# Scan block of a state-space layer: input products of two chunks interleaved, and 13 instead of 9 of 32 output products on GpSimd

## The chip, the core and the metric

The kernel runs on one core of a Trainium2 chip, in fp32 throughout. A core has five engines that run their own instruction queues beside each other: TensorE (PE in the profile) for matrix products into PSUM, VectorE (DVE), ScalarE (ACT), GpSimd (POOL), and SyncE (SP), which here only issues DMA transfers. GpSimd reads and writes SBUF alone; VectorE and ScalarE reach PSUM too in this kernel. The metric is the time of one execution on the device in microseconds (us), the median of three runs.

## The reference

The input is x of 4 batches x 512 tokens x 256 features and a context of 4 x 64 x 192. Four layers follow each other: two blocks with cross attention (the second with self attention too), a selective state-space stack (four "mamba" blocks after 64 tokens made of the context), and a last attention block. The change lies in the third. With 512 inner channels e and 16 states s, each of its blocks computes, after an input projection, a short convolution and a silu that give xi:

```python
dt, Bm, Cm = jnp.split(xdbl, [DR_, DR_ + DS_], axis=-1)
dt = jax.nn.softplus(jnp.einsum('bsr,er->bse', dt, dtp_w) + dtp_b)
A = -jnp.exp(A_log)
dA = jnp.exp(dt[..., None] * A)
dBu = dt[..., None] * Bm[:, :, None, :] * xi[..., None]

def step(h, t):
    da, dbu, c = t
    h = da * h + dbu
    return (h, jnp.einsum('bes,bs->be', h, c))
```

so for every channel and state there is a first-order recurrence over 512 tokens, and the output sums h times C over the states.

## The kernel before, in words

The state-space stack is `layer2` (from L1364). Its work is cut in 16 units (4 blocks x 4 batches). A unit has four chunks of 128 channels, taken as two pairs of chunks; the channels lie on the 128 partitions and the tokens along the row. A pair is done in 16 steps: a step i handles one chunk k of the pair and two states, and `where(i)` gives unit, pair, pair of states s2 and chunk k. Steps with the same s2 follow each other, so that two neighbouring steps (i even, i odd) share the maps of two states. In all there are 512 steps.

Parts of one step, with the engine that runs each:

- `maps` (L1674) has SP load B (tile bB) and C (tile bC) of two states, spread to all partitions, 512 KB each, once per two steps. bB has three buffers, bC four; bB is asked for five steps ahead, bC four.
- `product` (L1681) on GpSimd multiplies dtx (dt times xi, one chunk) by bB into dBu, 2 x 511 elements a row (L1685): dtx is read twice, once per state, and every row of bB once. dBu has four buffers.
- `decay` (L1689) on ScalarE writes exp(dt A) to PSUM (ps_dA, two buffers), one instruction per state (L1697).
- `begin` (L1699) on ScalarE copies the state at token 0 into column 0 of dBu (L1702), for each step.
- `states` (L1704) on VectorE scans 1024 elements (L1712), from ps_dA and dBu.
- The output product h times bC is done either by VectorE in the same step (`outputs_here`, L1719, tile hC) or by GpSimd one step later (`outputs`, L1723, tile hP). `on_gpsimd` (L119) says which: of 32 steps, 9 go to GpSimd.
- `add_up` on PE adds the products into ps_y by transposing matmuls (L1745), two steps behind or, for GpSimd's, three. After 16 steps `close_pair` (L1755) on VectorE multiplies the sum by the gate.

The rest of a unit (projections, convolution, gate, output projection) is written as generators (`front`, `step`, `gate`, `gated`) that are advanced twice a step. `step` (L1538) prepares a pair: dt for two chunks, then for each chunk dtx (L1564) and a small chain h0, i0 for token 0 (L1566 to L1575). The order on every engine is the order in which the loop at the end of `layer2` issues the instructions; nothing is moved afterwards. A buffer of a tile is written again only when its last reader is done, and an engine whose next instruction waits for that stands still with all that is behind it in its queue.

The context, ctxT, is loaded once at the start (L135) by ScalarE's queue into a tile that stays for the whole program; the first two layers, the state-space prefix and the last layer read it.

Of the kernel before, what the change touches and what calls it, by code (L numbers as in the profile page):

```python
# [8 lines left out]
F32 = mybir.dt.float32  # L9
# [6 lines left out]
P = 128  # L16
# [101 lines left out]

def on_gpsimd(i):  # L119

    return i % 4 == 0 or i % 32 == 26


@with_exitstack
def kernel(ctx: ExitStack, tc: tile.TileContext, t: dict, out: bass.AP):
# [5 lines left out]
    cols = keep.tile([P, NCOL], F32, name="cols")  # L131
    nc.scalar.dma_start(out=cols, in_=t["cols"])

    ctxT = keep.tile([CP, 2, B, 2, S], F32, name="ctxT")
    nc.scalar.dma_start(out=ctxT, in_=t["ctxT"].rearrange("(c p) b r s -> p c b r s", p=CP))  # L135
    const = keep.tile([P, 1 + TPB], F32, name="const")
    mean_w, mhalf = const[:, 0:1], const[:, 1:]
    nc.gpsimd.memset(mean_w, 1.0 / D)
# [1225 lines left out]
    def layer2(hT, A, far, h63, tail, X, fw, wl, late):  # L1364
# [5 lines left out]
        with ExitStack() as st:  # L1370
# [167 lines left out]
            def step(n, pair):  # L1538


                l, b = divmod(n, B)
                q = units[n]
                while "fronted" not in q:
                    yield
                w, xd, xi, b0 = q["w"], q["xd"], q["xi"], q["b0"]
                ms = (2 * pair, 2 * pair + 1)
                dt2 = pool.tile([P, 2, T], F32, name="dt", tag="dt", bufs=2)
                for i, m in enumerate(ms):
                    yield from need(1, 0)
# [10 lines left out]
                q["got", pair] = got = []  # L1560
                for i, m in enumerate(ms):
                    dt = dt2[:, i, :]
                    dtx = pool.tile([P, T], F32, name="dtx", tag="dtx", bufs=4)
                    nc.gpsimd.tensor_mul(dtx, dt, xi[:, m, :])  # L1564
                    h0 = pool.tile([P, NS], F32, name="h0", tag="h0", bufs=4)
                    nc.scalar.activation(h0, A[:, l, m, :], AF.Exp, scale=dt[:, 0:1])  # L1566
                    yield
                    yield
                    i0 = pool.tile([P, NS], F32, name="i0", tag="i0", bufs=2)
                    nc.gpsimd.tensor_mul(i0, b0, dtx[:, 0:1].broadcast_to([P, NS]))  # L1570
                    nc.gpsimd.tensor_mul(h0, h0, h63[:, l, b, m, :])
                    nc.gpsimd.tensor_add(h0, h0, i0)
                    yield
                    yield
                    nc.scalar.copy(dt[:, 0:1], far)  # L1575
                    q["used0"] = q.get("used0", 0) + 1
                    got.append((dt, dtx, h0))
                    yield

            def gate(n):  # L1580

# [92 lines left out]
            def maps(i, k):  # L1674

                n, pair, s2, _ = where(i)
                tl = pool.tile([P, 2, T], F32, name=("bB", "bC")[k], tag=("bB", "bC")[k], bufs=3 + k)
                nc.sync.dma_start(out=tl, in_=units[n]["scr"][k, 2 * s2 : 2 * s2 + 2].partition_broadcast(P))
                bmap[i // 2, k] = tl

            def product(i):  # L1681
                n, pair, s2, k = where(i)
                dtx = units[n]["got", pair][k][1]
                dBus[i] = dBu = pool.tile([P, 2, T], F32, name="dBu", tag="dBu", bufs=4)
                nc.gpsimd.tensor_mul(  # L1685
                    dBu[:, :, 1:], dtx[:, 1:].unsqueeze(1).broadcast_to([P, 2, T - 1]), bmap[i // 2, 0][:, :, 1:]
                )

            def decay(i, j):  # L1689
                n, pair, s2, k = where(i)  # L1690
                l, b = divmod(n, B)
                m, s = 2 * pair + k, 2 * s2 + j
                if j == 0:
                    dAs[i] = psum.tile([P, 2, T], F32, name="ps_dA", tag="dA", bufs=2)
                dA = dAs[i][:, j, :]
                dt = units[n]["got", pair][k][0]
                nc.scalar.activation(dA, dt, AF.Exp, scale=A[:, l, m, s : s + 1])  # L1697

            def begin(i):  # L1699
                n, pair, s2, k = where(i)  # L1700
                h0 = units[n]["got", pair][k][2]
                nc.scalar.copy(dBus[i][:, :, 0], h0[:, 2 * s2 : 2 * s2 + 2])  # L1702

            def states(i):  # L1704
                if on_gpsimd(i):
                    hC = pool.tile([P, 2, T], F32, name="hP", tag="hP", bufs=2)
                else:
                    hC = pool.tile([P, 2, T], F32, name="hC", tag="hC", bufs=4)
                hCs[i] = hC
                dA = dAs[i].rearrange("p s t -> p (s t)")  # L1710
                to = hC.rearrange("p s t -> p (s t)") if on_gpsimd(i) else dA
                nc.vector.tensor_tensor_scan(  # L1712
                    to, dA, dBus.pop(i).rearrange("p s t -> p (s t)"), 0.0, ALU.mult, ALU.add
                )

            def outputs_here(i):
                dA = dAs.pop(i)
# [64 lines left out]
            with tc.manual_schedule():  # L1782
                for i in range(first, last):
# [18 lines left out]
                    if main and r in (10, 14):  # L1802
                        flush_silu()

                    for k, ahead in ((0, 5), (1, 4)):
                        j = i + ahead
                        if 0 <= j < NU * US and j % 2 == 1:
                            maps(j - 1, k)
# [6 lines left out]
                    if i == -1:  # L1815
                        product(0)
                        product(1)
                        begin(0)
                    if main and i + 2 < NU * US:
                        product(i + 2)  # L1820
                    if 0 <= i - 1 < NU * US:
                        outputs(i - 1)

# [16 lines left out]
                        advance()  # L1840
                    if main:
                        outputs_here(i)
                    if 1 <= i + 2 < NU * US:
                        begin(i + 2)
                    if not closing:
                        advance()
# [126 lines left out]

    with ExitStack() as st:
        predram = st.enter_context(tc.tile_pool(name="prescr", bufs=2, space=DRAM))
        wp = st.enter_context(tc.tile_pool(name="w8", bufs=4))
        xp = st.enter_context(tc.tile_pool(name="X1", bufs=1))
        X = xp.tile([P, NT, D], F32, name="X")
        side = Beside(st.enter_context(ExitStack()))
        layer0(X, wp, side)  # L1980
        w = {n: load_l1(wp, n) for n in ("Wq1", "Wk1", "Wv1", "Wo1")}
        layer1(X, wp, w, st, side, hT)
    with ExitStack() as st:
# [15 lines left out]
        layer2(hT, A, far[:, 0:1], h63, tail, X, fw, wl, late)  # L1999
        layer3(X, wa, wl)  # L2000


# [68 lines left out]
```

## Time and profile before

| | before |
|---|---|
| median of 3 runs | 4056.72 us (4055.46 to 4058.05) |
| profiled execution, first to last instruction | 4054.1 us |
| scans of the main loop, first to last start | 1593.2 to 3337.8 us |
| busy in the span: PE, DVE, ACT, POOL | 3472.6, 3010.6, 2183.2, 2430.7 us |
| input products on GpSimd, L1685 | 512 of 2364 ns |
| output products on GpSimd, L1723 | 144 of 2360 ns |
| scans on VectorE, L1712 | 512 of 2.28 us |
| output products on VectorE, L1719 | 368 of 1223 ns |
| loads bB and bC | 256 each, 512 KB, 3.7 and 4.4 us to landing |

The profiled execution's own total time is not recorded beside its span; the span is 2.6 us below the median of the runs. A row of a group reads: line, engine, operation, output<-inputs with partitions x elements, number of instructions, then busy time and mean duration, then the time that the engine sat idle before them and who ended that. Durations of neighbouring instructions of one engine overlap by some hundredths of a microsecond.

### The profile page before, as it was taken

How to read it: one execution, taken by the hardware profiler on the slowest of the kernel's cores; microseconds unless marked ns; L12 is line 12 of the kernel's file. 1: busy time of each engine (PE TensorE's matmuls, PEld its weight loads, DVE VectorE, ACT ScalarE, POOL GpSimd, SP SyncE). 2: the span in 40 equal slices, each digit the busy share in tenths (PEclk: the TensorE clock that was granted, in tenths of full speed). 3: DMA queues.
4: the chain of work that ended last, by engine and by line, in shares of the span. 5: the costliest groups of instructions: out<-in, count | busy, mean ns of one | idle time of the engine just before them, and what ended most of it. 6: DMA issues, size and time to landing. Idle time of an engine off the chain costs nothing. (4 is left out here: it accounts for less than half of the span.)

```text
span 4054.1 us, 48619 instructions
## 1 busy us (share of the span) xinstructions
PE 3472.6 (86%) x17616; PEld 2197.1 (54%) x17616; DVE 3010.6 (74%) x2885; ACT 2183.2 (54%) x4394; POOL 2430.7 (60%) x1649
## 2 busy tenths in 40 slices
PE   7989998998888897887888798888887668999889
PEld 4654554554565554555555565555555444555446
DVE  5547567566565642899999999999999996666653
ACT  2345455454322433676777767776776644556422
POOL 3349259077100424899999999999999971001121
PEclk9999999999998998888888888888888779999989
DMA  2023023023100112444454445444444431000000
GB/s 77 12 91 101 26 79 99 18 89 105 45 1 0 56 28 85 151 152 160 155 175 159 163 155 169 164 167 148 161 171 147 168 109 37 1 1 1 1 6 16
DMA packets 140287, 369.93 MB, mean 91 GB/s; under 512 B 20624, under 2 KB 38224, under 8 KB 140048
## 3 DMA queue, kind: packets, MB, share of 16 engines
q1 hardware_dynamic: 136688, 363.58, 27.1%
q10 hardware_dynamic: 3360, 3.25, 0.3%
q8 instruction: 139, 2.28, 0.2%
q14 instruction: 100, 0.82, 0.1%
HBM read 363.50 MB, written 3.28 MB: 90 GB/s over the span
## 5 line engine op out<-in xcount | busy, mean ns | idle before, releaser
L1685 POOL TENSOR_TENSOR dBu<-dtx,bB 128x1022 f32<-128x1022 f32 x512 | 1200.7, 2364 | 14.7 <-DVE ps_dA L1712 12.4
L1697 ACT ACTIVATE ps_dA<-dt,A 128x512 f32<-128x512 f32 x1024 | 708.0, 691 | 390.6 <-DVE hC L1719 336.1
L1712 DVE TENSOR_TENSOR_SCAN ps_dA<-ps_dA,dBu 128x1024 f32<-128x1024 f32 x368 | 840.4, 2284 | 26.4 <-ACT ps_dA L1697 20.5
L1019 ACT ACTIVATE pr<-ps_s,nm 128x512 f32<-128x512 f32 x512 | 345.2, 686 | 259.2 <-DVE nm L1015 259.2
L1745 PE MATMUL ps_y<-ident,hC 128*128 128x128 f32 x2944 | 420.3, 294 | 56.7 <-DVE hC L1719 56.3
L1719 DVE TENSOR_TENSOR hC<-ps_dA,bC 128x1024 f32<-128x1024 f32 x368 | 450.2, 1223 | 21.7 <-DVE ps_dA L1712 0.5
L1745 PEld LDWEIGHTS ps_y<-ident,hC 128*128 128x128 f32 x2944 | 372.0, 153 | 119.6 <-DVE hC L1719 81.0
L1015 DVE TENSOR_REDUCE nm<-ps_s 128x2 f32<-128x1024 f32 x256 | 301.3, 1218 | 159.0 <-PE ps_s L1004 144.7
L1712 DVE TENSOR_TENSOR_SCAN hP<-ps_dA,dBu 128x1024 f32<-128x1024 f32 x144 | 328.4, 2280 | 52.7 <-POOL dBu L1685 48.1
L1723 POOL TENSOR_TENSOR hP<-hP,bC 128x1024 f32<-128x1024 f32 x144 | 339.9, 2360 | 26.5 <-PE ps_y L1745 9.8
L1033 PE MATMUL ps_pt<-ident,pr 128*128 128x128 f32 x2048 | 285.2, 279 | 66.6 <-DVE pT L1038 34.7
L1033 PEld LDWEIGHTS ps_pt<-ident,pr 128*128 128x128 f32 x2048 | 233.1, 142 | 164.9 <-issue 61.4
L663 POOL TENSOR_TENSOR ln_rstd<-ln_rstd,const 128x4 f32<-128x4 f32 x24 | 24.4, 1019 | 445.3 <-DVE ln_rstd L662 443.7
L582 DVE TENSOR_TENSOR_SCAN phb<-pdA,phb 128x512 f32<-128x512 f32 x128 | 224.5, 1768 | 62.3 <-POOL phb L572 45.8
L178 PE MATMUL ps_cv<-xp,w_dg 128*128 128x512 f32 x512 | 240.9, 607 | 28.9 <-ACT dBu L1702 21.6
L1745 PE MATMUL ps_y<-ident,hP 128*128 128x128 f32 x1152 | 188.6, 318 | 86.8 <-POOL hP L1723 86.8
L1745 PEld LDWEIGHTS ps_y<-ident,hP 128*128 128x128 f32 x1152 | 164.7, 167 | 144.1 <-POOL hP L1723 95.3
L1036 ACT COPY pT<-ps_pt 128x512 f32<-128x512 f32 x256 | 140.7, 592 | 171.6 <-PE ps_pt L1033 171.0
L1052 PE MATMUL ps_o<-pT,V 128*64 128x256 f32 (+1 forms) x2048 | 220.5, 392 | 1.8 <-ACT AT L1070 1.8
L1004 PE MATMUL ps_s<-kT,qT 64*128 64x512 f32 (+1 forms) x1024 | 207.5, 643 | 2.2 <-DVE kT L1225 1.4
L572 POOL TENSOR_TENSOR phb<-hT_res,pm 128x512 f32<-128x512 f32 x128 | 188.2, 1475 | 32.8 <-DMA pm<-scrp 18.1
L835 POOL TENSOR_TENSOR pr<-pr,rs 128x512 f32<-128x512 f32 x64 | 65.4, 1043 | 219.2 <-DVE rs L833 201.0
(275 smaller groups left out, 6408.6 us busy)
## 6 DMA issues: line engine op xcount, KB each, us to landing
bB<-scr SPq DMA_DIRECT2D x256, 512.0 KB, 3.7
bC<-scr SPq DMA_DIRECT2D x256, 512.0 KB, 4.4
pm<-scrp SPq DMA_DIRECT2D x224, 256.0 KB, 3.1
w_pw_in<-in_L_in SPq DMA_DIRECT2D x7, 512.0 KB, 4.5
X<-in_x SPq DMA_DIRECT2D x4, 512.0 KB, 7.2
w_L_W<-in_L_W SPq DMA_DIRECT2D x2, 1024.0 KB, 10.1
w_L_Wq<-in_L_Wq SPq DMA_DIRECT2D x2, 1024.0 KB, 6.5
w_L_Wo<-in_L_Wo SPq DMA_DIRECT2D x2, 1024.0 KB, 8.9
```

The costliest lines, as they stand in the source:

```text
L178: nc.tensor.matmul(dst, l, r, start=(i == 0), stop=(i == len(pairs) - 1))
L582: nc.vector.tensor_tensor_scan(hb, dA, hb, 0.0, ALU.mult, ALU.add)
L1015: nc.vector.tensor_reduce(nm, ps, AX.X, ALU.max, negate=True)
L1019: nc.scalar.activation(pr, ps[:, x, :], AF.Exp, bias=nm[:, x : x + 1], accum_out=rs[:, y : y + 1])
L1033: nc.tensor.transpose(pp[:, t4, :], pr[:, t4 * P : (t4 + 1) * P], ident)
L1052: nc.tensor.matmul(ps_o[0][j * stride : (j + 1) * stride, half * W2 : (half + 1) * W2], Vs[n][0][:, t4, h * stride : (h + 1) * stride], pT ...
L1685: nc.gpsimd.tensor_mul(dBu[:, :, 1:], dtx[:, 1:].unsqueeze(1).broadcast_to([P, 2, T - 1]), bmap[i // 2, 0][:, :, 1:])
L1697: nc.scalar.activation(dA, dt, AF.Exp, scale=A[:, l, m, s : s + 1])
L1712: nc.vector.tensor_tensor_scan(to, dA, dBus.pop(i).rearrange("p s t -> p (s t)"), 0.0, ALU.mult, ALU.add)
L1719: nc.vector.tensor_mul(hCs[i], dA, bmap[i // 2, 1])
L1723: nc.gpsimd.tensor_mul(hCs[i], hCs[i], bmap[i // 2, 1])
L1745: nc.tensor.matmul(y[:, j, k * P : (k + 1) * P], hC[:, s, j * P : (j + 1) * P], ident, is_transpose=True, start=False, stop=(2 * s2 + s == ...
```

## The change

`product` writes the two chunks of a pair into one tile dBu[state, token, chunk], the chunk innermost: one GpSimd instruction still covers 1022 elements, now both chunks of one state instead of both states of one chunk. dtx holds both chunks side by side for each token, and bB is read with each of its elements twice. `step` makes dtx, h0 and i0 for both chunks in single instructions (h0's two exponentials stay two). The scan reads its half of dBu with a step of two elements. `begin` copies once per two steps. Products are issued three steps ahead instead of two, dBu has three buffers of a pair (formerly four of a step), bB two buffers and is asked for six steps ahead. GpSimd takes the output products of all even steps but 10, 20 and 30 of 32: 13 instead of 9. hP and hC share six buffers (formerly two and four). ctxT no longer stays for the whole program: it is loaded at the start for the first layers, and again for the last one, first on SP's queue there.

```diff
 def on_gpsimd(i):
-    return i % 4 == 0 or i % 32 == 26
+    return i % 2 == 0 and i % 32 not in (10, 20, 30)
...
-    ctxT = keep.tile([CP, 2, B, 2, S], F32, name="ctxT")
-    nc.scalar.dma_start(out=ctxT, in_=t["ctxT"].rearrange("(c p) b r s -> p c b r s", p=CP))
+    def load_contexts(pool, queue):
+        nonlocal ctxT
+        ctxT = pool.tile([CP, 2, B, 2, S], F32, name="ctxT")
+        queue.dma_start(out=ctxT, in_=t["ctxT"].rearrange("(c p) b r s -> p c b r s", p=CP))
...
+                dtx = pool.tile([P, T, 2], F32, name="dtx", tag="dtx", bufs=2)
+                nc.gpsimd.tensor_mul(dtx.rearrange("p t k -> p k t"), dt2, xi[:, ms[0] : ms[1] + 1, :])
+                h0 = pool.tile([P, 2, NS], F32, name="h0", tag="h0", bufs=2)
                 for i, m in enumerate(ms):
-                    dt = dt2[:, i, :]
-                    dtx = pool.tile([P, T], F32, name="dtx", tag="dtx", bufs=4)
-                    nc.gpsimd.tensor_mul(dtx, dt, xi[:, m, :])
-                    h0 = pool.tile([P, NS], F32, name="h0", tag="h0", bufs=4)
-                    nc.scalar.activation(h0, A[:, l, m, :], AF.Exp, scale=dt[:, 0:1])
...
+                    nc.scalar.activation(h0[:, i, :], A[:, l, m, :], AF.Exp, scale=dt2[:, i, 0:1])
...
+                i0 = pool.tile([P, 2, NS], F32, name="i0", tag="i0")
+                nc.gpsimd.tensor_mul(
+                    i0, b0.unsqueeze(1).broadcast_to([P, 2, NS]), dtx[:, 0, :].unsqueeze(2).broadcast_to([P, 2, NS])
+                )
+                nc.gpsimd.tensor_mul(h0, h0, h63[:, l, b, ms[0] : ms[1] + 1, :])
+                nc.gpsimd.tensor_add(h0, h0, i0)
...
             def maps(i, k):
...
-                tl = pool.tile([P, 2, T], F32, name=("bB", "bC")[k], tag=("bB", "bC")[k], bufs=3 + k)
+                tl = pool.tile([P, 2, T], F32, name=("bB", "bC")[k], tag=("bB", "bC")[k], bufs=2 + 2 * k)
...
             def product(i):
-                n, pair, s2, k = where(i)
-                dtx = units[n]["got", pair][k][1]
-                dBus[i] = dBu = pool.tile([P, 2, T], F32, name="dBu", tag="dBu", bufs=4)
+                n, pair, s2, j = where(i)
+                dtx = units[n]["got", pair][1]
+                if j == 0:
+                    dBus[i // 2] = pool.tile([P, 2, T, 2], F32, name="dBu", tag="dBu", bufs=3)
                 nc.gpsimd.tensor_mul(
-                    dBu[:, :, 1:], dtx[:, 1:].unsqueeze(1).broadcast_to([P, 2, T - 1]), bmap[i // 2, 0][:, :, 1:]
+                    dBus[i // 2][:, j, 1:, :],
+                    dtx[:, 1:, :],
+                    bmap[i // 2, 0][:, j, 1:].unsqueeze(2).broadcast_to([P, T - 1, 2]),
                 )
...
             def begin(i):
-                nc.scalar.copy(dBus[i][:, :, 0], h0[:, 2 * s2 : 2 * s2 + 2])
+                nc.scalar.copy(dBus[i // 2][:, :, 0, :], h0[:, :, 2 * s2 : 2 * s2 + 2].rearrange("p k s -> p s k"))
...
             def states(i):
-                if on_gpsimd(i):
-                    hC = pool.tile([P, 2, T], F32, name="hP", tag="hP", bufs=2)
-                else:
-                    hC = pool.tile([P, 2, T], F32, name="hC", tag="hC", bufs=4)
-                hCs[i] = hC
+                hCs[i] = hC = pool.tile([P, 2, T], F32, name="hP" if on_gpsimd(i) else "hC", tag="hC", bufs=6)
...
-                nc.vector.tensor_tensor_scan(
-                    to, dA, dBus.pop(i).rearrange("p s t -> p (s t)"), 0.0, ALU.mult, ALU.add
-                )
+                dBu = dBus[i // 2].rearrange("p s t k -> p (s t) k")[:, :, i % 2]
+                nc.vector.tensor_tensor_scan(to, dA, dBu, 0.0, ALU.mult, ALU.add)
...
-                    for k, ahead in ((0, 5), (1, 4)):
+                    for k, ahead in ((0, 6), (1, 4)):
...
-                    if main and i + 2 < NU * US:
-                        product(i + 2)
+                    if main and i + 3 < NU * US:
+                        product(i + 3)
...
-                    if 1 <= i + 2 < NU * US:
+                    if main and i % 2 == 0 and i + 2 < NU * US:
                         begin(i + 2)
...
     def layer3(X, wa, wl):
...
+            load_contexts(wp, nc.sync)
...
+        load_contexts(st.enter_context(tc.tile_pool(name="contexts", bufs=1)), nc.scalar)
```

More of the change, by code (lines that the diff above doesn't have):

```diff
@@ L132 @@
     nc.scalar.dma_start(out=cols, in_=t["cols"])
-    ctxT = keep.tile([CP, 2, B, 2, S], F32, name="ctxT")
-    nc.scalar.dma_start(out=ctxT, in_=t["ctxT"].rearrange("(c p) b r s -> p c b r s", p=CP))
+    ctxT = None
+    def load_contexts(pool, queue):
+        nonlocal ctxT
+        ctxT = pool.tile([CP, 2, B, 2, S], F32, name="ctxT")
+        queue.dma_start(out=ctxT, in_=t["ctxT"].rearrange("(c p) b r s -> p c b r s", p=CP))
     const = keep.tile([P, 1 + TPB], F32, name="const")
@@ L1559, in step @@
                     q["sized"] = True
-                q["got", pair] = got = []
+                dtx = pool.tile([P, T, 2], F32, name="dtx", tag="dtx", bufs=2)
+                nc.gpsimd.tensor_mul(dtx.rearrange("p t k -> p k t"), dt2, xi[:, ms[0] : ms[1] + 1, :])
+                h0 = pool.tile([P, 2, NS], F32, name="h0", tag="h0", bufs=2)
                 for i, m in enumerate(ms):
-                    dt = dt2[:, i, :]
-                    dtx = pool.tile([P, T], F32, name="dtx", tag="dtx", bufs=4)
-                    nc.gpsimd.tensor_mul(dtx, dt, xi[:, m, :])
-                    h0 = pool.tile([P, NS], F32, name="h0", tag="h0", bufs=4)
-                    nc.scalar.activation(h0, A[:, l, m, :], AF.Exp, scale=dt[:, 0:1])
[L1567 to L1578, printed above, removed]
+                    nc.scalar.activation(h0[:, i, :], A[:, l, m, :], AF.Exp, scale=dt2[:, i, 0:1])
+                yield
+                yield
+                yield
+                i0 = pool.tile([P, 2, NS], F32, name="i0", tag="i0")
[4 more added lines that the diff above has]
+                nc.gpsimd.tensor_add(h0, h0, i0)
+                yield
+                yield
+                nc.scalar.copy(dt2[:, :, 0], far)
+                q["used0"] = q.get("used0", 0) + 2
+                q["got", pair] = dt2, dtx, h0
+                yield
             def gate(n):
@@ L1695, in decay @@
                 dA = dAs[i][:, j, :]
-                dt = units[n]["got", pair][k][0]
+                dt = units[n]["got", pair][0][:, k, :]
                 nc.scalar.activation(dA, dt, AF.Exp, scale=A[:, l, m, s : s + 1])
@@ L1700, in begin @@
                 n, pair, s2, k = where(i)
-                h0 = units[n]["got", pair][k][2]
-                nc.scalar.copy(dBus[i][:, :, 0], h0[:, 2 * s2 : 2 * s2 + 2])
+                h0 = units[n]["got", pair][2]
+                nc.scalar.copy(dBus[i // 2][:, :, 0, :], h0[:, :, 2 * s2 : 2 * s2 + 2].rearrange("p k s -> p s k"))
             def states(i):
-                if on_gpsimd(i):
-                    hC = pool.tile([P, 2, T], F32, name="hP", tag="hP", bufs=2)
-                else:
-                    hC = pool.tile([P, 2, T], F32, name="hC", tag="hC", bufs=4)
-                hCs[i] = hC
+                hCs[i] = hC = pool.tile([P, 2, T], F32, name="hP" if on_gpsimd(i) else "hC", tag="hC", bufs=6)
                 dA = dAs[i].rearrange("p s t -> p (s t)")
                 to = hC.rearrange("p s t -> p (s t)") if on_gpsimd(i) else dA
-                nc.vector.tensor_tensor_scan(
-                    to, dA, dBus.pop(i).rearrange("p s t -> p (s t)"), 0.0, ALU.mult, ALU.add
-                )
+                dBu = dBus[i // 2].rearrange("p s t k -> p (s t) k")[:, :, i % 2]
+                nc.vector.tensor_tensor_scan(to, dA, dBu, 0.0, ALU.mult, ALU.add)
             def outputs_here(i):
@@ L1817, in layer2 @@
                         product(1)
+                        product(2)
                         begin(0)
-                    if main and i + 2 < NU * US:
-                        product(i + 2)
+                    if main and i + 3 < NU * US:
+                        product(i + 3)
                     if 0 <= i - 1 < NU * US:
@@ L1997, in late @@
                 nc.sync.dma_start(out=wa[n], in_=t[f"L3_{n}"].rearrange("(c p) n -> p c n", p=P))
-        layer2(hT, A, far[:, 0:1], h63, tail, X, fw, wl, late)
+        layer2(hT, A, far[:, 0:2], h63, tail, X, fw, wl, late)
         layer3(X, wa, wl)
```

## The prediction

> **What bounds the kernel now.** First the page's slices: from the 16th to the 33rd of 40, VectorE and GpSimd are both at nine tenths while ScalarE is at seven. That stretch is the scan block, the only code that the change rewrites.
>
> ```profile
> PE   7989998998888897887888798888887668999889
> DVE  5547567566565642899999999999999996666653
> ACT  2345455454322433676777767776776644556422
> POOL 3349259077100424899999999999999971001121
> ```
>
> Then the busy time by windows of 100 us inside it (the columns after the length are PE, PE weight loads, DVE, ACT, POOL, clock, DMA share, GB/s):
>
> ```profile
> 2000.00:2100.00 100.00, 82.23 (x400) 54.85 (x398) 97.99 (x59) 72.51 (x130) 98.95 (x58) 0.92 0.54 177
> 2100.00:2200.00 100.00, 85.06 (x410) 58.42 (x410) 97.99 (x59) 71.72 (x131) 99.21 (x60) 0.91 0.49 160
> 2200.00:2300.00 100.00, 86.75 (x408) 59.87 (x409) 97.80 (x61) 73.79 (x134) 98.48 (x61) 0.88 0.49 161
> 2300.00:2400.00 100.00, 85.49 (x380) 56.59 (x379) 92.22 (x56) 66.31 (x123) 99.22 (x64) 0.86 0.46 154
> ```
>
> Over the sixteen windows from 1700 to 3300 us GpSimd is busy 1551 us and VectorE 1544 us. So both bound it at once; relieving one alone buys little. Third, the groups of instructions of these two engines in that same stretch, by shape:
>
> ```profile
> L1712 DVE TENSOR_TENSOR_SCAN ps_dA<-ps_dA,dBu 128x1024 f32<-128x1024 f32 x341 | 778.6, 2283 | 14.1 <-ACT ps_dA L1697 9.9 <-POOL dBu L1685 2.7 <-ACT dBu L1702 1.2
> L1719 DVE TENSOR_TENSOR hC<-ps_dA,bC 128x1024 f32<-128x1024 f32 x341 | 417.2, 1223 | 20.2 <-DVE ps_dA L1712 0.5 <-PE ps_y L1745 0.5
> L1712 DVE TENSOR_TENSOR_SCAN hP<-ps_dA,dBu 128x1024 f32<-128x1024 f32 x133 | 303.3, 2280 | 1.8 <-ACT xp L1496 1.3 <-ACT dBu L1702 0.4
> ...
> L1685 POOL TENSOR_TENSOR dBu<-dtx,bB 128x1022 f32<-128x1022 f32 x474 | 1111.5, 2364 | 8.4 <-DVE ps_dA L1712 6.1 <-DMA bB<-scr 2.2
> L1723 POOL TENSOR_TENSOR hP<-hP,bC 128x1024 f32<-128x1024 f32 x133 | 313.8, 2360 | 23.0 <-PE ps_y L1745 9.8 <-ACT dBu L1702 7.5 <-DVE hP L1712 3.2
> L1564 POOL TENSOR_TENSOR dtx<-dt,xi 128x512 f32<-128x512 f32 x58 | 73.9, 1274 | 6.8 <-ACT dt L1362 5.6 <-ACT dBu L1702 1.2
> L1447 POOL TENSOR_TENSOR w_dg<-ident,cols 128x512 f32<-128x512 f32 x12 | 12.5, 1042 | 0.0
> ```
>
> The same kind of product with a repeated second input, over the whole span:
>
> ```profile
> L835 POOL TENSOR_TENSOR pr<-pr,rs 128x512 f32<-128x512 f32 x64 | 65.4, 1043 | 219.2 <-DVE rs L833 201.0
> ```
>
> The reader is to see: 474 scans in 1600 us are 3.376 us a step, 108.0 us a unit of 32 steps. 1600 us are 14.8 units, so a unit has 104.7 us of GpSimd and 104.3 us of VectorE, and 3.3 and 3.7 us idle. Nobody else's waiting is large in these rows.
>
> **The change part by part.** Instructions of one engine overlap a little in the records: four products in a row take 9.31 us in the timeline, 2.33 us each beside the 2.364 of the row. I price a step by what it adds in a row.
>
> *Four more output products by GpSimd* (13 of 32, not 9): +4 x 2.32 = +9.3 us of GpSimd a unit. VectorE loses four L1719. In the timeline a pair of steps with one output product on VectorE starts every 5.70 us (2120.15, 2125.85, 2131.55), and a single step that has its own takes 3.46 (2137.20, 2140.66). So a pair without GpSimd's help is 6.92, and -1.22 x 4 = -4.9 us: VectorE goes from 104.3 to 99.4 us a unit.
>
> *Input products in the new order.* 32 instructions of the same 1022 elements; only the patterns differ: dtx and dBu run contiguously over (t, chunk), and the map bB is read with each element twice, that is with a step of zero inside a run of two. No row has runs of two. The two ends:
> Without a saving it stays 2.36 us, as L1685 and L1723 (1022 and 1024 elements, two streams of fresh values).
> With the saving of the rows whose second input has step zero in its inner run: L1447 (4 runs of 128) takes 1042 ns for 512 elements, L835 over the whole span (8 runs of 64) 1043 ns, against 1274 ns for L1564, 512 elements of two fresh streams. From 1274 at 512 and 2364 at 1022 an element costs 2.14 ns and the instruction 180 ns, so a repeated second input costs (1042 - 180)/512 = 1.68 ns an element, and 1022 elements 1.90 us.
> In between, if each fresh map value pays the difference (511 values instead of 1022), 2.13 us.
> Above 2.36: L835 has four runs more than L1447 and takes 1 ns more, 0.25 ns a run, and 511 runs would be 0.13 us: 2.49 at worst.
> I take 1.95: the access that it is nearest to in form is that of L835 and L1447 (first input and output contiguous, second with step zero), and between runs of 64 and of 128 the saving does not depend on the length; 0.05 is for the turns. That is -0.41 x 32 = -13.1 us of GpSimd a unit.
>
> [...]
>
> *dtx, h0, i0 for both chunks at once.* Four dtx of 1.27 become two of 1024 elements, some 2.36 each as L1723: -0.4 us. Twelve small ones of 0.22 become six; with 32 elements 0.25 by the slope: -1.1 us. dtx is now written with a step of two elements, which no GpSimd row has: between 2.36 and double, +4.7 us a unit at worst; taken at 2.36, since L1723 is the nearest (same length, same engine). Nothing covers it: GpSimd is left level with VectorE, so a doubling would cost 75 us in 16 units.
>
> Sum for GpSimd: 104.7 + 9.3 - 13.1 - 1.5 = 99.4 us a unit, level with VectorE's 99.4.
>
> *The scan reads dBu with a step of two elements.* No DVE row has that. A scan costs 2.28 us for 1024 elements, L1719 1.22 with one contiguous SBUF input: the scan takes in an element at about half the rate at which this engine is shown to read, so a read of half the rate still feeds it. Bounds: no cost, or at most a doubling to 4.6 us, as the prefix scans L582 (512 elements) have from 1.19 to 2.29 us beside a busy GpSimd. I take nothing, being nearer to the unchanged scan (same operation, one input in PSUM).
> [...]
>
> *begin once per pair*: 16 ScalarE copies of 0.18 us fewer a unit; ScalarE is idle a quarter of the time, so nothing. It writes after the pair's second product, which is one step later than now, and products are issued one step earlier: no change of lead.
>
> *bB with two buffers, asked for six steps ahead.* Now a load may start when the products of three pairs before are done, afterwards when those of two before are done. SP then issues (0.32 us) and it lands 3.7 us later (3.3 to 9.1): 4.1 us. Meanwhile GpSimd does two products and one output product, 2 x 1.9 + 2.3 = 6.1 us, without the output (3 pairs of 16) 3.8. Behind it in SP's queue stand bC, b0 and the weight loads. At a layer change three or four loads of up to 512 KB go ahead of it; if each costs 2 us, 3 x 4 x 2 = 24 us, and 3 x 0.3 a unit is 14 us. Bounds 0 to +38; I take +8, because in the three-pair gaps VectorE has two output products more to do and is the later one.
>
> *hP and hC share six buffers*: removes the 9.8 us in which L1723 waited for PE's transposes; counted at nothing, as others wait then.
>
> *ctxT in two places.* At the start it is issued behind cols on ScalarE's queue, where it was. For the last layer 384 KB go first on SP's queue, near 3361 us; w_L_ck is wanted by the contexts' ps_k at 3699 us. More than 300 us of cover; without it about 4 us.
>
> Sum: a unit is 99.4 us of both plus the idle of today's worse one, 3.7, = 103.1, that is 4.9 less than 108.0; 16 units: -78. With +8 for bB: -70. The profiled execution spans 4054.1 us and the median of the three runs is 4056.72, so 2.6 lie around it: 4054.1 - 70 + 2.6 = 3987 us.
>
> **The rivals.**
> *The repeat saves nothing* (product 2.36). GpSimd has 104.7 + 9.3 - 1.5 = 112.5 us a unit, and with 2 to 3.3 idle 114.5 to 115.8: +6.5 to 7.8 a unit, 4160 to 4182 us. For it: the rows with a saving have long runs. Against: they save as much at 64 as at 128. It ends slower than before as soon as a product takes more than 2.14 us (104.7 reached again).
> *Half the saving* (2.13): GpSimd 105.1; with VectorE no longer level and idle down to about 2.5, 107.6: -6 us, and bB's +8 cancels it: 4030 to 4070. That the rows show only the ends speaks for it.
> *The strided read slows the scan.* Each 0.1 us a scan is 3.2 us a unit or 51 us in all; from 0.14 us on the gain is gone. [...] Against: the scan's low appetite.
> *bB and dtx both cost*: the loads' +38 in full (30 more than taken) and half of dtx's 75: about 4055.
>
> **How the numbers follow.** Near-full saving 0.57 (3955 to 4025), half 0.15, no saving 0.13, slow scan 0.10, loads or dtx 0.05. Below 3950 I leave 0.03, above 4140 0.17: range 3950 to 4140; the likeliest one's own 3955 to 4025. 0.2% is 8 us, about what a measurement here can tell. Faster: 0.57 + 0.08 of the half case + 0.03 = 0.68; same 0.05 (half case, loads); slower 0.27.
>
> **What would show it.** The input products' row at 1.9 to 2.0 us instead of 2.36 (wrong: 2.1 or more); the scan's rows still near 2.28; 304 output products on VectorE and 208 on GpSimd; both engines still at nine tenths, the block some 1675 us long instead of 1745. In the waits, DMA bB before the products below 15 us. A DVE row of scans at 2.4 us or more, or GpSimd alone at 9 and VectorE at 8 tenths, would make the forecast wrong.

## The result, and the profile after

The changed kernel takes 4067.83 us (median of 6 runs, 4062.98 to 4076.77) against 4056.09 us (6 runs, 4051.91 to 4059.45): a ratio of 1.0028 (95% interval 1.0017 to 1.004). It is slower by 0.28%, where the forecast was 3987 us, faster by 1.7%. The time lies in the range 3950 to 4140, outside the likeliest part of it (3955 to 4025) and inside that of the rival "half the saving" (4030 to 4070). The profiled execution took 4068.3 us with a span of 4066.5.

The page's slices of the changed kernel, 40 of equal length, busy share in tenths:

```profile
PE   7989998998888897888888888888888568999889
DVE  5547567566565642889999989999999995676653
ACT  2345455454322433666767767666676643566422
POOL 3349269077100424899999999999999981000131
```

GpSimd is still at nine tenths throughout the block; VectorE has one more slice at eight. The windows of 100 us say more (after the length: PE, PE weight loads, DVE, ACT, POOL, clock, DMA share, GB/s):

```profile
2000.00:2100.00 100.00, 85.14 (x399) 56.77 (x399) 91.77 (x55) 68.09 (x111) 98.18 (x56) 0.89 0.48 164
2100.00:2200.00 100.00, 86.99 (x407) 58.61 (x408) 93.22 (x56) 70.09 (x114) 97.38 (x55) 0.89 0.50 164
2200.00:2300.00 100.00, 89.57 (x408) 59.75 (x408) 92.67 (x55) 69.99 (x114) 98.74 (x56) 0.86 0.48 156
2300.00:2400.00 100.00, 83.28 (x374) 55.49 (x375) 90.17 (x53) 67.46 (x112) 99.42 (x60) 0.86 0.49 156
```

VectorE falls from 98 to 92 us in 100, as its work was taken away, and GpSimd stays at 97 to 99. The groups of these two engines between 1700 and 3300 us:

```profile
L1718 DVE TENSOR_TENSOR_SCAN ps_dA<-ps_dA,dBu 128x1024 f32<-128x1024 f32 x280 | 639.1, 2283 | 59.8 <-ACT ps_dA L1706 57.0 <-POOL dBu L1692 2.5
L1718 DVE TENSOR_TENSOR_SCAN hP<-ps_dA,dBu 128x1024 f32<-128x1024 f32 x192 | 437.6, 2279 | 1.0 <-POOL dBu L1692 0.3 <-PE ps_y L1749 0.3 <-ACT xp L1501 0.3
L1633 DVE TENSOR_TENSOR hT_res<-ps_out,hT_res 128x512 f32<-128x512 f32 x30 | 20.7, 692 | 39.6 <-PE ps_out L183 39.6
...
L1692 POOL TENSOR_TENSOR dBu<-dtx,bB 128x1022 f32<-128x1022 f32 x472 | 999.6, 2135 | 4.8 <-issue 2.6 <-DVE ps_dA L1718 1.1 <-DMA bB<-scr 0.4
L1727 POOL TENSOR_TENSOR hP<-hP,bC 128x1024 f32<-128x1024 f32 x193 | 456.4, 2365 | 20.4 <-DVE hP L1718 20.2
L1566 POOL TENSOR_TENSOR dtx<-dt,xi 128x1024 f32<-128x1024 f32 x29 | 68.7, 2369 | 8.0 <-ACT dt L1367 8.0
```

Three things are to be seen. The input product takes 2.135 us, not 1.95. The scan is unchanged. And VectorE, with less to do, has two new waits: before ps_dA 57.0 us for ScalarE, and before ps_out's addition 39.6 us for TensorE. The view of VectorE's waits in the same stretch, first of the kernel before:

```profile
DVE ps_dA L1712 <- ACT ps_dA L1697: 9.9, 21, 0.6
DVE hT_res L1627 <- PE ps_out L178: 5.8, 10, 0.8
```

and then of the changed one (total us, times, longest us):

```profile
DVE ps_dA L1718 <- ACT ps_dA L1706: 57.0, 58, 2.4
DVE hT_res L1633 <- PE ps_out L183: 39.6, 30, 2.6
```

472 scans in these 1600 us are 108.5 us a unit, against 108.0 (one scan more or less in the stretch is 0.2 us a unit). A unit is now 105.7 us of GpSimd (1559.4 / 14.75) and 99.8 us of VectorE. VectorE's busy time fell by 72 us in these windows, and the two waits grew by 81. The first scan starts 4.8 us later (1593.17 and 1597.97 us; the first dtx alone starts 3.1 later), and the loop, first to last start, grew from 1744.6 to 1753.6 us.

### The profile page after: what moved, and what is told of

Its sections match the earlier page's. It is cut to its first block, busy times and chain, and to the rows that moved or that the text cites. A ratio compares the mean times of both kernels' runs of the same rounds, so it can differ in the third digit from the quotient of the medians.

```text
span 4066.5 us, 48201 instructions
## 1 busy us (share of the span) xinstructions
PE 3492.8 (86%) x17616; PEld 2200.1 (54%) x17616; DVE 2942.0 (72%) x2821; ACT 2156.9 (53%) x4106; POOL 2440.9 (60%) x1585
## 3 DMA queue, kind: packets, MB, share of 16 engines
q8 instruction: 139, 2.28, 0.2%
## 5 line engine op out<-in xcount | busy, mean ns | idle before, releaser
L1692 POOL TENSOR_TENSOR dBu<-dtx,bB 128x1022 f32<-128x1022 f32 x512 | 1084.7, 2136 | 13.0 <-DVE ps_dA L1718 5.9
L1706 ACT ACTIVATE ps_dA<-dt,A 128x512 f32<-128x512 f32 x1024 | 710.7, 694 | 358.1 <-DVE hC L1723 306.9
L1718 DVE TENSOR_TENSOR_SCAN ps_dA<-ps_dA,dBu 128x1024 f32<-128x1024 f32 x304 | 693.9, 2283 | 72.3 <-ACT ps_dA L1706 69.4
L1718 DVE TENSOR_TENSOR_SCAN hP<-ps_dA,dBu 128x1024 f32<-128x1024 f32 x208 | 474.1, 2279 | 58.9 <-POOL dBu L1692 49.8
L1727 POOL TENSOR_TENSOR hP<-hP,bC 128x1024 f32<-128x1024 f32 x208 | 491.9, 2365 | 26.9 <-DVE hP L1718 26.8
L1723 DVE TENSOR_TENSOR hC<-ps_dA,bC 128x1024 f32<-128x1024 f32 x304 | 371.7, 1223 | 17.9 <-PE ps_in L190 0.4
L1749 PE MATMUL ps_y<-ident,hC 128*128 128x128 f32 x2432 | 354.4, 296 | 27.3 <-DVE hC L1723 27.1
L1749 PE MATMUL ps_y<-ident,hP 128*128 128x128 f32 x1664 | 263.2, 311 | 110.7 <-POOL hP L1727 110.5
L1749 PEld LDWEIGHTS ps_y<-ident,hC 128*128 128x128 f32 x2432 | 309.9, 154 | 66.9 <-DVE hC L1723 41.8
L1749 PEld LDWEIGHTS ps_y<-ident,hP 128*128 128x128 f32 x1664 | 227.5, 162 | 198.2 <-POOL hP L1727 140.7
```

The costliest lines, as they stand in the source:

```text
L1692: nc.gpsimd.tensor_mul(dBus[i // 2][:, j, 1:, :], dtx[:, 1:, :], bmap[i // 2, 0][:, j, 1:].unsqueeze(2).broadcast_to([P, T - 1, 2]),)
L1718: nc.vector.tensor_tensor_scan(to, dA, dBu, 0.0, ALU.mult, ALU.add)
L1723: nc.vector.tensor_mul(hCs[i], dA, bmap[i // 2, 1])
L1727: nc.gpsimd.tensor_mul(hCs[i], hCs[i], bmap[i // 2, 1])
L1749: nc.tensor.matmul(y[:, j, k * P : (k + 1) * P], hC[:, s, j * P : (j + 1) * P], ident, is_transpose=True, start=False, stop=(2 * s2 + s == ...
```

## The experiments

Two questions: why the product costs 2.135 us, and whether that price is why the gain did not come. Edits are against the changed kernel unless another is named. "The windows" are those from 1700 to 3300 us; ratios are to the kernel before in the same comparison.

**The price alone.** e4_micro appends a stretch of measurement behind the kernel (its time is added):

```diff
+        for r in (1, 2, 4, 8, 16, 64, 256, 1024):
+            rep = b[:, : N // r].unsqueeze(2).broadcast_to([P, N // r, r])
+            for _ in range(4):
+                nc.gpsimd.tensor_mul(o.rearrange("p (n r) -> p n r", r=r), a.rearrange("p (n r) -> p n r", r=r), rep)
...
+                nc.vector.tensor_tensor_scan(o, d, src, 0.0, ALU.mult, ALU.add)   # src in steps of 1, 2, 3, 4
...
+                nc.vector.tensor_mul(o, d, src)                                   # src in steps of 1, 2, 4
```

> The changed kernel with a measurement behind it, on idle engines: GpSimd products of 1024 elements whose second input has runs of 1, 2, 4, 8, 16, 64, 256 and 1024 equal elements, four of each; the first input with runs of two, both inputs with runs of two, a product with one constant; VectorE scans and products with PSUM and an SBUF input of step 1, 2, 3, 4. Theory A (a fresh element of the second input costs its share): 2.36, 2.14, 2.02, 1.96, 1.93 and 1.91 us from there on; both inputs with runs of two 1.9. Rival C (a pair of equal elements is special, or each run costs a turn): 2.14 at two, and 1.90 at once from four on, or the runs of four and eight near 2.14 too. [...]

The total was 4164.03 us. The timeline of GpSimd there (start, duration), one product of 1024 elements each with the second input in runs of 1, 2, 4, 8, 16, 64 and 256, then both inputs in runs of two:

```profile
4073.38 2.34 POOL L2021 TENSOR_TENSOR run<-ma,mb 128x1024 f32<-128x1024 f32 x1
4075.68 2.12 POOL L2021 TENSOR_TENSOR run<-ma,mb 128x1024 f32<-128x1024 f32 x1
...
4090.93 2.00 POOL L2021 TENSOR_TENSOR run<-ma,mb 128x1024 f32<-128x1024 f32 x1
4092.89 1.96 POOL L2021 TENSOR_TENSOR run<-ma,mb 128x1024 f32<-128x1024 f32 x1
...
4106.47 1.93 POOL L2021 TENSOR_TENSOR run<-ma,mb 128x1024 f32<-128x1024 f32 x1
4108.36 1.90 POOL L2021 TENSOR_TENSOR run<-ma,mb 128x1024 f32<-128x1024 f32 x1
...
4121.47 1.89 POOL L2021 TENSOR_TENSOR run<-ma,mb 128x1024 f32<-128x1024 f32 x1
...
4138.37 2.11 POOL L2031 TENSOR_TENSOR both<-ma,mb 128x1024 f32<-128x1024 f32 x1
```

Within 0.02 us a product is 1.89 + 0.45/r us for runs of r: 2.12 for r = 2, 2.00 for 4. Each fresh value of the repeated input pays the same there, some 0.44 ns (0.45 us in 1024). The expected 1.9 for both inputs in runs of two failed: 2.11, no better than one. VectorE's scan took 2.27 to 2.29 us at every step of its SBUF input, and its product 1.23, 1.23 and 1.97 us at steps of 1, 2 and 4.

**The saving in full, in the kernel.** e2_zero13 gives the product one map element for the whole row, so that its second input is never fresh (so the recurrence gets another input):

```diff
-                    bmap[i // 2, 0][:, j, 1:].unsqueeze(2).broadcast_to([P, T - 1, 2]),
+                    bmap[i // 2, 0][:, j, 0:1].unsqueeze(2).broadcast_to([P, T - 1, 2]),
```

> The changed kernel (13 of 32) with the input products reading one map value 1022 times (step zero everywhere) instead of each value twice; so the recurrence gets a wrong input, everything else is as in the changed kernel. Theory A: the product falls to 1.90 us, GpSimd to 105.7 - 32 x 0.235 = 98.2 us a unit, VectorE at 99.8 is the bound, 102.8 us with idle time: 5.7 x 16 = 91 us less than the changed kernel, about 3977 us; that would show that the sum of the prediction held but for this price. Rival B (begin or bB): at most half of that comes, 4020 us or more, although the product is at 1.90.

4056.64 us, ratio 1.0001 (0.9989 to 1.0012). This is the central experiment: a product still cheaper than forecast gives back 11 us and no more. Its product group, its windows in one row, and VectorE's waits:

```profile
L1692 POOL TENSOR_TENSOR dBu<-dtx,bB 128x1022 f32<-128x1022 f32 x479 | 900.2, 1895 | 40.2 <-DVE ps_dA L1718 34.2 <-DMA bB<-scr 3.4 <-issue 2.6
```
```profile
1700.00:3300.00 1600.00, 1323.48 (x6237) 897.09 (x6236) 1483.66 (x873) 1103.54 (x1783) 1463.20 (x875) 0.88 0.48 162
```
```profile
DVE ps_dA L1718 <- ACT ps_dA L1706: 53.6, 57, 2.0
DVE hT_res L1633 <- PE ps_out L183: 35.5, 30, 2.7
```

VectorE is busy 1484 of 1600 us and GpSimd 1463: neither is full, and GpSimd now waits for VectorE. A unit is 107.3 us with 99.5 of VectorE and 7.8 of its idle, where the forecast carried over 3.7. The same two waits hold 89 of its 116 idle us.

**The old product with 13 of 32.** e3_old13 is the kernel before with only the new line:

```diff
-    return i % 4 == 0 or i % 32 == 26
+    return i % 2 == 0 and i % 32 not in (10, 20, 30)
```

> The kernel before with 13 instead of 9 of 32 output products on GpSimd and nothing else changed. Theory A: GpSimd has 104.7 + 9.3 = 114.0 us a unit and bounds it alone; with 2 to 2.8 us idle 116 to 117, that is 8 to 9 us more than 108.0: 4185 to 4200 us. Rival B (the other edits of the change cost something of their own, and the cheaper input product gives less than 7 us a unit): under 4150 us.

4150.02 us, ratio 1.023 (1.0209 to 1.0251). GpSimd is busy 1592.2 of 1600 us and a unit is 114.8 us, 114.2 of them GpSimd: with the price of 2.36 the forecast's sum for GpSimd (104.7 + 9.3) is met to 0.2 us. The estimate for the time was 35 to 50 us too high, in good part because only half a us a unit stays idle where 2 to 2.8 were taken.

**How many output products.** Other counts, with the rest of the change:

```diff
-    return i % 2 == 0 and i % 32 not in (10, 20, 30)
+    return i % 4 == 0 or i % 32 == 26                            # e7_g9
+    return i % 4 == 0 or i % 32 in (6, 26)                       # e16_g10
+    return i % 4 == 0 or i % 32 in (6, 22, 26)                   # e17_g11_quads
+    return i % 2 == 0 and i % 32 not in (4, 10, 18, 24, 30)      # e1_g11
```

> The changed kernel with 11 of 32 output products on GpSimd (even steps but 4, 10, 18, 24, 30). Theory A (only the price of the new input product was mis-sized: 2.14 us, not 1.95): a unit has 105.7 - 2 x 2.33 = 101.0 us of GpSimd and 99.8 + 2 x 1.22 = 102.2 us of VectorE, level again; with 2.8 us idle 105.0 instead of 108.5 us: 16 x 3.5 = 56 us less than the changed kernel, about 4012 us. Rival B (ScalarE's begin, which waits for the pair's second product and holds the decays behind it, or bB's two buffers, is what holds the loop): the balance does not matter, 4050 to 4070 us, and VectorE's wait for ps_dA stays at 57 us or more in the window from 1700 to 3300 us.

> The changed kernel with the 9 of 32 output products of the kernel before, on the same steps. GpSimd would have 105.7 - 9.3 = 96.4 us a unit, VectorE 99.8 + 4.9 = 104.7 with its waits covered as in the kernel before. Theory D: VectorE bounds it alone, 104.7 + 3.5 idle = 108.2: the same as before, 4050 to 4060 us, and the wait for ps_dA near 10 us. Rival B (the other edits cost something of their own: begin, bB's buffers): 4070 us or more. Theory A (only the balance of the two engines): 4040 us or less.

> The changed kernel with 10 of 32: the nine steps of the kernel before and step 6; VectorE keeps 2, 10, 14, 18, 22 and 30. GpSimd 98.7, VectorE 103.5 us a unit. If most of VectorE's cover at ScalarE's bursts stays, its idle time stays at 3.5 to 4 us a unit: 107.0 to 107.5, about 4040 us, and this is the best right kernel. If taking the product from step 6 uncovers TensorE's backlog there: 4050 to 4056 us, with more than 20 us of waiting for ps_out in the window from 1700 to 3300 us.

> 11 of 32: the nine steps of the kernel before and 6 and 22. GpSimd 101.0, VectorE 102.2 us a unit; VectorE keeps 2, 10, 14, 18 and 30, so four of the five bursts are covered, and GpSimd has 6 and 8, 20 to 28 in a row. Cover theory: VectorE's wait for ps_dA under 25 us against 46 us of the other 11 of 32, idle 5 us a unit, 4045 to 4052 us. If uneven load on GpSimd decides: 4060 us or more.

| of 32 | time, us | ratio | VectorE busy in the windows | GpSimd busy | wait for ps_dA | for ps_out |
|---|---|---|---|---|---|---|
| 9 (e7) | 4052.16 | 0.9989 (0.9979 to 0.9998) | 1549 | 1439 | 11 | 9 |
| 10 (e16) | 4044.80 | 0.9979 (0.9969 to 0.9988) | 1539 | 1478 | 9 | 22 |
| 11 (e17) | 4056.13 | 1.0007 (0.9997 to 1.0017) | 1516 | 1503 | 26 | 25 |
| 11 (e1) | 4058.03 | 1.0005 (0.9995 to 1.0015) | 1505 | 1497 | 48 | 12 |
| 13 (after) | 4067.83 | 1.0028 (1.0017 to 1.004) | 1472 | 1559 | 57 | 40 |

Row 9 shows that the rest of the change costs nothing on balance and that it, the cheaper product above all, frees 111 us of GpSimd, which no one uses: VectorE is the bound there. From 9 to 11, VectorE's busy time falls (by 44 us in e1) and its two waits rise by about as much (39), while GpSimd has 100 us to spare. So it was not GpSimd's load that kept 11 from the expected 4012 us. e16_g10 is 0.2% faster than the kernel before and 0.5% faster than the changed one; its interval still overlaps that of 9 of 32, and 12 was not tried.

**Where VectorE's own products stand.** The theory: an own output product of VectorE (1.22 us) right where ScalarE is late would cover it.

```diff
-    return i % 2 == 0 and i % 32 not in (10, 20, 30)
+    return i % 2 == 0 and i % 32 not in (2, 6, 10, 14, 18)       # e5_g11_own
+    return i % 2 == 0 and i % 32 not in (2, 14, 18)              # e6_zero13_own, with e2's product
+    return i % 2 == 0 and i % 32 not in (2, 8, 14, 18, 24)       # e11_g11_spread
```

> 11 of 32 again, but VectorE keeps the even steps 2, 6, 10, 14 and 18, those in which ScalarE's table loads with softplus (steps 2 and 18) and silu (10 and 14) or TensorE's work after a pair is closed (6) fall, as in the kernel before. Theory D (VectorE waits at these steps because its step there has become shorter than ScalarE's burst and TensorE's backlog): VectorE's wait for ps_dA falls from 46 us to under 15 us in the window from 1700 to 3300 us, and a unit from 108.2 to about 105.9 us: some 4020 us. Rival E (ScalarE's and TensorE's work per unit bounds the loop wherever the products are): 4050 to 4060 us, the waits only move.

> 13 of 32 with the input product that reads one map value (1.90 us, wrong input to the recurrence), with VectorE keeping steps 2, 14 and 18 in place of 10, 20 and 30. Theory D: of the 54 us that VectorE waits for ps_dA most goes, the 36 us for ps_out stay: some 4010 us against 4056.64. Rival E: 4050 us or more.

> 11 of 32 with VectorE keeping 2, 8, 14, 18 and 24: under the bursts of ScalarE at 2, 14 and 18, but never more than six steps in a row alike, unlike the run that kept 2, 6, 10, 14, 18 and took 4084.97 us because GpSimd had ten steps with little and then twelve with much. Theory D (place of VectorE's own steps decides): wait for ps_dA under 25 us, 4035 us. Theory G: 4050 to 4065 us.

4084.97 us (1.0068, 1.0053 to 1.0083), 4040.81 (0.9959, 0.9945 to 0.9974) and 4065.75 (1.0036, 1.0023 to 1.005). With the product of e2, the place is worth 16 us, less than theory D's 46, and the wait for ps_dA is 46 us against 54; with the real one both tries are worse than e1. In e5 the wait for ps_dA fell to 24 us, as the theory wants, and the time rose. e5's other waits show the price of uneven loading, VectorE for PE's sum and for GpSimd's products:

```profile
DVE g L1765 <- PE ps_y L1749: 31.4, 3, 10.5
DVE ps_dA L1718 <- POOL dBu L1692: 15.9, 3, 5.3
```

The theory falls as a remedy; that ScalarE's lateness costs something is not refuted by it.

**Orders of issue.** Three more suspects: PE's additions wait for GpSimd's hP at the head of PE's queue (add them a step later); ScalarE's `begin` stands before the decays (a step later); the gate's matmuls come in a bunch with the closing of a pair (two steps later).

```diff
-                    for j in (i - 3, i - 2):
-                        if 0 <= j < NU * US and on_gpsimd(j) == (j == i - 3):
+                    for j in (i - 4, i - 3, i - 2):               # e8_zero13_lag with e2's product, e9_g11_lag with e1's line
+                        lag = 2 if not on_gpsimd(j) else 3 if j % 16 in (0, 14) else 4
+                        if 0 <= j < NU * US and j == i - lag:
...
-                    if main and i % 2 == 0 and i + 2 < NU * US:
-                        begin(i + 2)
+                    if main and i % 2 == 1 and i + 1 < NU * US:   # e10_g11_begin, with e1's line
+                        begin(i + 1)
...
-                    if 0 <= n < NU and r == LAG + 1:
+                    if 0 <= n < NU and r == LAG + 3:              # e15_g11_lag_gate, on top of e9
```

> As the run with 13 of 32 and an input product of 1.90 us (one map value, wrong input to the recurrence; 4056.64 us), but TensorE adds GpSimd's output products four steps behind instead of three (three still for steps 0 and 14 of a pair). Theory F (TensorE, in order, stands still for GpSimd's late products, 93 us in the window from 1700 to 3300 us; that makes ps_out and the evictions late, ScalarE behind them, and VectorE waits 54 us for ps_dA and 36 us for ps_out): TensorE's wait falls under 45 us, VectorE's two under 50 together, time about 4020 us. Rival G (TensorE's and ScalarE's bunched work between the closing of a pair and its tenth step holds VectorE, whatever the order): within 8 us of 4056.64, the waits only change their names.

> 11 of 32 (VectorE keeps 4, 10, 18, 24, 30) with GpSimd's products added four steps behind instead of three, output right. Without that edit 4058.03 us. Theory F: about 4025 us, TensorE's wait for hP from 90 to under 45 us. Rival G: within 8 us of 4058.

> 11 of 32 (VectorE keeps 4, 10, 18, 24, 30) with ScalarE's begin issued one step later, where the pair's second product is done. Theory B (begin waits for that product and holds the decays behind it): VectorE's wait for ps_dA falls from 46 us to under 20, time about 4030 us. Theories F and G: within 8 us of 4058.03, the wait stays above 35 us.

> 11 of 32 (VectorE keeps 4, 10, 18, 24, 30), GpSimd's products added four steps behind, and the gate's projection begun two steps later in a unit (step 5, not 3), so that less of TensorE's work falls on the first steps after the closing; output right. Without the last edit 4055.01 us. Theory G: 1 to 2 us a unit, 4025 to 4040 us. Rival H: within 8 us of 4055.

4055.48 us (1.0007, 0.9998 to 1.0017), 4055.01 (1.0003, 0.9994 to 1.0012), 4078.63 (1.0072, 1.0055 to 1.0089) and 4127.75 (1.0171, 1.0155 to 1.0187). The first two leave the time where it was: in e2's product version PE had waited 92.5 us for hP and 34.5 for hC; with the lag it waits 109.3 for hC. So this wait of PE does not set the time. What did change is VectorE's two waits in e8 (53.6 and 35.5 us in e2):

```profile
DVE ps_dA L1718 <- ACT ps_dA L1706: 70.5, 66, 2.7
DVE hT_res L1633 <- PE ps_out L183: 11.5, 15, 2.1
```

The wait for ps_out lost 24 us, that for ps_dA took 17 more, and no time was won: the waits changed their names, as rival G had said. So the length of a wait was here not what its removal brought. The later `begin` makes a new wait for dBu, 27.9 us, before VectorE's scans, so its lead is needed. With the later gate VectorE waits 78.7 us for ps_dA and 41.0 for ps_out, up to 6.9 at once: a worse place for TensorE's work.

**Less work for TensorE.** Half of the matmuls of two projections are left out (their sums cover half of the terms), in the version of e2, in the changed kernel and in the kernel before:

```diff
-  ... for c in range(DC)])     # ps_z
+  ... for c in range(1)])
-  ... for m in range(EC)])     # ps_out
+  ... for m in range(2)])
```

> As the run with 13 of 32 and an input product of 1.90 us (4056.64 us; wrong input to the recurrence), and besides half of TensorE's matmuls of the gate (ps_z) and of the output projection (ps_out) left out, so the sums are wrong there too; 7 us of TensorE a unit less, all of it in the ten steps after a unit's first pair is closed. Theory G (TensorE's bunched work there, 33 us in ten steps, holds ScalarE and VectorE): 4 to 6 us a unit less, 3965 to 3995 us. Rival H (the three engines lose that time to each other through their few buffers, and TensorE is only one that waits): within 15 us of 4056.

> The changed kernel with the same half of ps_z's and ps_out's matmuls left out (wrong gate and projection). GpSimd has 105.7 us of work a unit of 108.5. If that bounds it, at most 2 us a unit come: 4035 to 4065 us. If TensorE holds this kernel too: under 4015 us.

> The kernel before with the same half of ps_z's and ps_out's matmuls left out (wrong gate and projection). GpSimd has 104.7 and VectorE 104.3 us a unit of 108.0. Theory G: at most 2 us a unit, 4025 to 4055 us, far less than in the run with the cheap input product. If TensorE was the bound all along: under 4005 us.

4014.01 us (0.9888, 0.9871 to 0.9904), 4038.24 (0.9953, 0.9938 to 0.9968) and 4054.23 (0.999, 0.9981 to 1.0): -43, -30 and -2 us by the medians, -46, -30 and -4 by the ratios. The kernel before gains next to nothing, so its TensorE work was hidden; in the changed one it is not, up to the 30 us at which GpSimd is full (1574.5 of 1600 us busy in e13, and a time in the range that was stated for GpSimd as the bound). e12 lies between the ranges of theory G and of rival H. In it the wait for ps_out is gone, ScalarE's wait for ps_z has fallen from 63 to 6 us (1700 to 3200 us), and VectorE's wait for ps_dA remains:

```profile
DVE ps_dA L1718 <- ACT ps_dA L1706: 57.9, 59, 2.0
```

**No change of ScalarE's function table.** e12, with softplus replaced by a square and silu by a copy (so neither function is computed), which use no other table than the decays: at the lines of the decays, softplus and silu (L1706, L1367, L1780) e12 has 130 table loads in the whole run and e18 none; on every engine the order of all else stays:

```diff
-        nc.scalar.activation(dst, src, AF.Softplus, bias=bias)
+        nc.scalar.activation(dst, src, AF.Square, bias=bias)
...
-                    nc.scalar.activation(r, r, AF.Silu)
+                    nc.scalar.activation(r, r, AF.Identity)
```

> The run with the repeated map element and half of two projections' matmuls left out (4014.01 us; unit 105.8 us; VectorE waits 57.9 us for ps_dA in the sixteen windows), and ScalarE's function table is never changed inside the block: softplus is replaced by a square and silu by a copy (wrong values; same sizes and number of instructions). That takes about 116 table loads of 1.28 us, 149 us, from ScalarE in the sixteen windows; every other engine's instructions stay in the same order. Theory S, that the rest of the excess over the forecast's unit of 103.1 us is ScalarE's table changes, each of which leaves VectorE without a ps_dA: the wait for ps_dA falls below 15 us, the unit to 102.5-103.5 us, the time to 3965-3980. Rival R, that the wait for ps_dA only shows where a loop through several engines happens to stand, and another takes its place: the wait for ps_dA falls, but those for PE or for GpSimd grow, and the time stays at 4000 or above. In between, both have a part.

3947.83 us (0.9733, 0.9717 to 0.9749), 66 us less than e12 (63 by the ratios). The wait for ps_dA falls from 57.9 to 9.1 us and no other takes its place; the block ended earlier, so the views are of 1700 to 3200 us, windows first, then VectorE's waits:

```profile
1700.00:3200.00 1500.00, 1206.36 (x5915) 844.72 (x5913) 1458.54 (x865) 946.55 (x1654) 1437.50 (x860) 0.87 0.52 171
```
```profile
DVE g L1765 <- PE ps_y L1749: 9.3, 3, 3.1
DVE ps_dA L1718 <- ACT ps_dA L1706: 9.1, 13, 1.1
```

470 scans in 1500 us are 102.1 us a unit: VectorE 99.3 and 2.8 idle. In the same stretch e12 has 105.5 and e2 107.1. The scan loop is 56 us shorter than e12's (1646.9 against 1703.1), and it began 16 us earlier; that part, which nobody expected, makes the time lower than the 3965 to 3980 of theory S. The edit reaches ahead of the loop too: up to 1610 us ScalarE has 45 table loads where e12 has 56.

## Why the prediction was wrong

**The step that failed** is the last of the sum: "a unit is 99.4 us of both plus the idle of today's worse one, 3.7, = 103.1". The 99.4 of VectorE came (99.8 in the changed kernel, 99.5 in e2), the idle did not: 7.8 us in e2, with GpSimd below VectorE's load. That is 4.2 us a unit, 67 us of e2's miss of 70 (4056.6 against 3987); by the length of the loop, 1738.8 us against the forecast's 1675, it is 64. The idle of 3.7 belonged to a VectorE that did 23 own output products in 32 steps. They had covered two other engines, and four of them were taken away: for TensorE e14 against e12 and e13 shows it, for ScalarE it is argued from the wait for ps_dA, 9.9 us before and 57.0 after. e18 has the forecast's loads with both of these relieved, and its idle is 2.8: the busy sums were right, and the missing part is these two. What e18 takes out is more than the change had uncovered, so it shows where the idle came from and not what each engine's part of it is.

**TensorE.** After a pair is closed it works off a backlog almost without a pause (0.7 us idle in 20). The timeline of PE in e2:

```profile
2052.40 3.78 PE L1738 MATMUL ps_y<-w_dD,xi 128*128 128x128 f32 x16 [3.71 <-DVE g L1765]
2055.97 1.33 PE L1749 MATMUL ps_y<-ident,hP 128*128 128x128 f32 x8
...
2065.30 1.88 PE L190 MATMUL ps_z<-w_inz,hn 128*128 128x512 f32 x4
2067.02 3.60 PE L183 MATMUL ps_out<-gT,w_out 128*128 128x512 f32 x8
2070.45 1.88 PE L190 MATMUL ps_z<-w_inz,hn 128*128 128x512 f32 x4
```

and VectorE beside it:

```profile
2066.21 2.27 DVE L1718 TENSOR_TENSOR_SCAN ps_dA<-ps_dA,dBu 128x1024 f32<-128x1024 f32 x1
2070.66 0.69 DVE L1633 TENSOR_TENSOR hT_res<-ps_out,hT_res 128x512 f32<-128x512 f32 x1 [2.17 <-PE ps_out L183]
```

VectorE reaches the addition of ps_out 2.17 us before ps_out is done; all its scans stand behind it. That TensorE has a share is shown by e12, e13 and e14 (-43, -30, -2 us).

**ScalarE.** Its timeline in e2, where a silu changes the function table and back:

```profile
2089.97 1.28 ACT L1780 ACT_TABLE_LOAD   x1
2091.26 1.91 ACT L1780 ACTIVATE zs<-zs 128x2048 f32<-128x2048 f32 x1
2093.19 1.28 ACT L1706 ACT_TABLE_LOAD   x1
2094.49 1.42 ACT L1706 ACTIVATE ps_dA<-dt,A 128x512 f32<-128x512 f32 x2
```

4.5 us pass before the next decays, with two buffers of ps_dA, and VectorE's next scan comes late:

```profile
2095.93 2.30 DVE L1718 TENSOR_TENSOR_SCAN ps_dA<-ps_dA,dBu 128x1024 f32<-128x1024 f32 x1 [1.73 <-ACT ps_dA L1706]
```

A step of VectorE without an own product asks for one every 2.28 us, one with it every 3.5 (2.28 and 1.22). ScalarE is busy only 69% of the time, which in the forecast stood for "nothing". e18 shows its share: 56 us of the loop, once TensorE is relieved. That the length of these bursts does it, and not the 149 us less of ScalarE's work as such, is argued from this timeline. How the two engines split when both are present, and what the kernel before would gain without table changes, was not tried; with 104.7 us of GpSimd in its unit of 108.0 that would be at most 3.3 us a unit.

**The mis-sized term** is the input product, 2.135 instead of 1.95 us: it costs 11 us (4067.83 against 4056.64). The bound in between, 2.13 if each fresh map value pays the difference, was worked out and given 0.15; the choice of "nearest in form" compared runs of 64 with runs of 128, where the law of e4 (0.45/r) differs by 0.004 us and can tell nothing about r = 2. In e4 two fresh inputs of 1024 elements took 2.34 us and a second input in runs of 256 took 1.89.

**The rival that came nearest**, half the saving, had GpSimd at 105.1 (105.7 measured) and the unit at 107.6 (108.5). It was right in its price and in GpSimd as the fuller engine. What it does not hold is that a cheaper product would have brought 11 us only (e2): VectorE's waits stood right behind.

**A cost not counted**: from the first dtx to the first scan 8.2 us pass, 6.5 before. The other 3.1 of the 4.8 us by which the loop starts later are no cost of the change that the runs show: e3, which has the old code there, starts its first dtx at 1594.1 us, 7.4 later than the kernel before.

**Right**: -4.9 us a unit on VectorE (104.3 to 99.8, that is -4.5, and 99.5 in e2); +9.3 on GpSimd (e3); dtx for two chunks at 2.37 us, not doubled; the scan unhurt by its step of two (2283 ns before and after). e4 measured 2.27 to 2.29 us for it at steps of 1, 2, 3 and 4, while VectorE's product cost more at a step of 4 (1.97 us, 1.92 ns an element, against 1.23 us at steps of 1 and 2). The loads of bB cost less than the 8 us taken (2 us a load at a layer change, behind its upper bound, was an assumption that no run shows): products waited 0.4 us for them. Of the signs that it had written down, "2.1 or more" for the product's row did show it wrong.

**A slip that changed nothing**: the slices in which both engines stand at nine tenths are the 18th to the 32nd.

## What to carry to other kernels

Idle time of the bounding engine was here not a constant to be added to a smaller sum (3.7 us a unit before, 7.8 in e2): when work is taken off it, ask at each point where it meets another engine how late that one is, and how long a burst of that one lasts against its buffers, whatever its mean load. Here the price between two measured forms came per fresh value (2.13 us worked out, 2.135 measured), not from the form that looked nearest (1.95). And before a gain is credited to one cost, make that cost smaller than it can be (here a product with one map element): it showed at once that 13 of 32 at these steps would not pay even so; the series of counts then put 10 in front.

## What the runs showed of the hardware

In e4_micro GpSimd's product of two fp32 inputs of 1024 elements took 1.89 us plus 0.45 us times the share of its second input that was fresh (2.34 us with all of it fresh, 2.12 at runs of two, 2.00 at runs of four); a repeated first input saved the same (2.13 at runs of two), both repeated no more (2.11). VectorE's scan of 1024 elements took 2.27 to 2.29 us there whether its SBUF input came in steps of 1, 2, 3 or 4 elements.
